# Cross-attention with layer norm on one Trainium2 core: the mask conversion on GpSimd in pieces, other staging of the weights, and another order of the end

## The chip, the cores and the metric

The kernel runs on one core of a Trainium2 chip. A core has five engines with instruction queues of their own: PE (TensorE, matmuls; its weight loads are shown as PEld), DVE (VectorE), ACT (ScalarE), POOL (GpSimd) and SP (SyncE, which here only issues transfers). Each engine works through its queue in order, and semaphores tie the queues together. Sixteen DMA engines move data between the main memory (HBM), the on-chip memory (SBUF) and within SBUF. PE writes its results to PSUM, which has 8 banks here. The metric is the device time of one execution in microseconds.

## What is computed

```python
qs = (x @ wq) split into 16 heads of 32        # x: 4 x 2048 x 512
ks, vs = ctx @ wk, ctx @ wv                    # ctx: 4 x 77 x 512
scores = einsum("bhqd,bhkd->bhqk", qs, ks) / sqrt(32)
scores = where(mask, -inf, scores)             # mask: 4 x 2048 x 77
attn = softmax(scores) @ vs                    # heads joined again
out = attn @ wo + x
return (out - mean) / sqrt(var + 1e-5) * gamma + beta
```

All tensors are float32, the mask is one byte for each query and key. A query whose 77 keys are all masked must come out as NaN.

## The kernel before

**Tiles.** The 8192 queries are 64 tiles of 128 rows, 16 tiles a batch. Two tiles make a block (32 blocks, each with one attention-times-values group), four tiles a group for the query projection (16 groups). Keys are 77 wide, or 96 (NK2) with a copy of the last 19 so that two neighbouring heads can lie at different offsets.

**Precision.** Projections are done as three products of a high and a low part (`split`: ACT rounds the high part, DVE or GpSimd subtracts). So x, wq, wk, wo, wv, the context and the attention output all exist as high and low tiles.

**The main loop.** One period (`PERIOD`, lines 45 to 50) is a list of words that is recorded once for each p from 0 to 29; each word names an operation and, behind the colon, its lag. One period handles two tiles: two Q visits on PE (`Q`, line 168, 12 matmuls each) with their evacuation by DVE (`q`, line 185), scores of two tiles (`S`, line 291), maxima with the mask bias added (`T`, DVE, line 305, four quarters a tile), exponentials (`e`, ACT, line 319), reciprocals (`r`, DVE, line 330), normalisation (`n`, POOL, line 335), transposes into a B buffer (`t`, DVE, line 359), regrouping of B into PT by twelve DMAs a block (`P`, line 371, parts 0 to 11, in this loop all on SP), attention times values (`V`, line 385), its high and low parts (`a`, ACT, line 416; `b`, DVE, line 420), output projection (`O`, line 440), residual (`+`, DVE, line 449), statistics (`s`, lines 454 to 457), inverse deviation (`v`, POOL, lines 463 to 466), scaling (`k`, ACT), gamma and beta (`f`, POOL, lines 476 and 477) and store (`w`, SP). `g`, `i` and `j` load, round (ACT, line 157) and subtract (POOL, line 161) the transposed x of a group; `x` loads x for the residual.

**Extras.** The dictionary `extra` (lines 608 to 622) hangs further calls behind a word of a certain period: values projections, splits of wv and wo, and the mask. `load_mask` (line 263) fetches a batch's mask bytes into m8, which has one buffer, and takes the bias tile mb (two buffers). `mask_bias` (line 270) turns the bytes into a bias of -3e38 or 0 in bf16: one DVE multiplication, line 272, and a DVE copy of the 19 repeated columns, line 273. `mask_nan` (line 275) reduces the mask to one value a query that is NaN where all keys are masked, lines 277 to 279. For batch m the first tiles run in period p = 2 + 8m; the load hangs at p - 3, the two halves of the bias at p - 2 and p - 1, the NaN row at p - 1. Batch 0 is loaded at the start; its bias is made in three slices (lines 555, 610 and 611), its NaN row in period 5.

**Buffers.** The staging tiles stage_a and stage_b and all PT tiles share the tag PT (two buffers); ctx_f, ctx_h (context as loaded, and its high part) and all B tiles share the tag B (two buffers). stage_a takes wq and wk, then xT of group 1; stage_b takes wv and wo. ctx_h is read by the keys and the values projections.

**Order.** The kernel is recorded under a manual schedule: each engine's queue holds its instructions in the order in which the words and extras call them. After period 29 the string `ORDER` (lines 52 to 72) takes over and lists the rest word by word, with the queue of each regroup transfer (s SP, g GpSimd, a ACT). There, `U` is a regroup of a single tile, `X` adds the residual by an identity matmul on PE (line 429) in place of `+`, and `u`, `y`, `z` are the steps of the layer norm for one tile.

```python
 extra[p - 3, "S0"] = [(load_mask, m)]
 extra[p - 2, "T1.1"] = [(mask_bias, m, slice(0, half))]
 extra[p - 1, "T1.1"] = [(mask_bias, m, slice(half, TPB)), (mask_nan, m)]
```

Of the kernel before, what the change touches and what calls it, by code (L numbers as in the profile page):

```python
# [57 lines left out]
P27.0s n56 Q60 q61 e57.1 P27.5s T58.3 P27.6s b25.1 e58.3 q62 P27.11g T58.2 S59 u48 x55 e57.3 t56 Q63 P27.1g
e58.2 r57 T59.0 n57 T59.1 e59.0 q60 T59.2 V26 e59.1 f46 T59.3 t57 e58.1 O50 q63 P28.4g a26.0 w46 z48 a26.1
P28.8s P28.7g b26.0 e58.0 P28.10g P28.0s z49 S60 P28.3g b26.1 e59.2 P28.2g +50 O53 P28.6g x54 r58 T60.1 w49 n58  # L60
e59.3 w48 T60.3 P28.9s T60.0 e60.3 T60.2 S61 t58 e60.1 X51 x57 P28.11s r59 T61.2 n59 e60.0 V27 P28.1s T61.0
P28.5s T61.1 e61.2 +53 O51 t59 e60.2 T61.3 P29.3g P29.11s s50 x56 S62 P29.2s a27.0 r60 u50 s51 e61.1 P29.8s O52
T62.0 P29.6s u51 b27.0 a27.1 P29.10s e61.3 T62.1 P29.9s P29.0g y51 b27.1 n60 e61.0 V28 +52 T62.2 r61 S63 T62.3
P29.4g a28.0 t60 a28.1 n61 X55 e62.1 b28.0 O55 P29.5a s52 e62.2 t61 u52 X54 e62.3 P29.7g b28.1 P30.2s P30.3g z51
X57 P30.8s P29.1g P30.4a T63.2 P30.1s O54 y52 P30.6s e62.0 T63.3 P30.11s T63.0 P30.0s e63.3 y50 w51 O57 r62 z50
P30.10s P30.7a T63.1 n62 w50 s53 e63.0 s54 V29 x59 P30.9a P30.5g z52 e63.1 t62 u53 O56 a29.1 y53 U62.5g U62.9s
U62.10a h63.0 U62.8s s55 m63.0 e63.2 x58 b29.1 w52 V30 z53 a29.0 h63.1 w53 U62.3a y55 s57 m63.1 U62.4a X59 b29.0
u55 a30.1 t63 a30.0 O59 U62.0a x61 y57 U63.6g U63.4s U62.11a y54 U62.1s U63.1a b30.0 u54 U62.6s O58 +56 U63.11s
U63.9a U63.10g b30.1 U63.5a U63.7g x60 z55 U63.3g z54 w55 O61 U63.0s s56 u57 U63.2s +58 U63.8g U62.7s z57 U62.2s
s58 u56 O60 x63 w54 +61 u58 s59 s61 u59 W63 +60 u61 x62 s60 W62 c63 w57 y59 X63 c62 d63 u60 d62 O63 y61 y58 z61  # L70
y60 X62 y56 z60 O62 z58 w60 w61 z56 w58 s63 z59 s62 u63 w59 w56 y63 u62 y62 z63 z62 w63 w62
"""


# [1 line left out]
def xattn_layernorm(  # L76
# [186 lines left out]
    def load_mask(b):
        m8 = sb.tile([P, TPB, NK], U8, tag="m8", bufs=1, name=f"m8_{b}")
        nc.sync.dma_start(m8, mask[b])
        mb = sb.tile([P, TPB, NK2], BF16, tag="mb", name=f"mb_{b}")
        nz = sb.tile([P, TPB], F32, tag="nz", name=f"nz_{b}")
        bat[b] = (mb, nz, m8)

    def mask_bias(b, ts=slice(0, TPB)):  # L270
        mb, nz, m8 = bat[b]
        nc.vector.tensor_scalar(mb[:, ts, TAIL_K:], m8[:, ts], MASKED, None, ALU.mult)
        nc.vector.tensor_copy(mb[:, ts, :TAIL_K], mb[:, ts, NK:])

    def mask_nan(b):
        mb, nz, m8 = bat[b]
        nc.vector.tensor_reduce(nz, m8, AX.X, ALU.min)
# [274 lines left out]
    for c in range(0, NC_D, 2):  # L552
        split(*(a[:, c : c + 2, BLK:] for a in gx[0]), f0[c][:, 1])
    q_visit(0, 0)
    mask_bias(0, slice(0, 1))
    gate(stage_a[:, 1, NC_D - 1, D - 1 :])
    load_wv()
    for m in range(0, NG, 2):
        keys_evac(pks, m)
# [58 lines left out]
    for m in range(1, NB):
        p = 2 + m * half
        extra[p - 3, "S0"] = [(load_mask, m)]  # L620
        extra[p - 2, "T1.1"] = [(mask_bias, m, slice(0, half))]
# [65 lines left out]
```

## Time and profile before

| | |
|---|---|
| median of 3 runs | 549.29 us (548.66 to 549.4) |
| the profiled execution | 549.31 us, its span 547.5 us |
| mean granted clock of PE | 0.982 of full speed |
| ACT, exponentials, 1024 (line 319) | 352.7 us busy, 351 ns each |
| DVE, maxima, 1024 (line 305) | 170.5 us busy, 232 ns each |
| DVE, transposes, 64 (line 359) | 96.2 us busy, 1503 ns each |
| POOL, normalisation, 63 (line 335) | 142.6 us busy, 2264 ns each |
| DVE, mask bias, 616 elements (line 272) | 6 of 770 ns |
| DVE, mask bias, 152 elements (line 273) | 6 of 1188 ns |
| DVE, NaN reduction (line 277) | 4 of 1421 ns |

The span runs from the first to the last instruction of the program in one execution; the execution's own time is a little longer. Busy time is the union of an engine's instructions. In the tables by stage, each row is one stretch of the span: its length, then the busy time of each engine in it with the number of instructions, then the mean granted clock of PE and the share of the DMA engines. In the timeline, each line has the start, the duration, the engine ("SPq" is SP's queue issuing transfers), the line of the kernel, what is written and read, how many, and in brackets the idle time of the engine before it and what ended it.

### The profile page before, as it was taken

What the parts mean: (1) busy time and instruction counts of PE and PEld (TensorE: products, weight loads), DVE (VectorE), ACT (ScalarE), POOL (GpSimd) and SP (SyncE); (2) the same over time, 40 slices, a digit from 0 to 9 for tenths busy, and PEclk for the clock granted to TensorE, in tenths of its full rate; (3) what the DMA queues carried; (4) which work ended last, traced back from release to release, by engine and by line L of the source; (5) the groups of instructions that cost most, each with busy time, mean ns of one, the idle gap of its engine ahead of it and who ended that gap; (6) DMA issues with size and microseconds to landing.
All of it is one profiled execution on the core that took longest, in us unless ns stands there. A gap on an engine that the chain in (4) does not pass through costs nothing.

```text
span 547.5 us, 16162 instructions
## 1 busy us (share of the span) xinstructions
PE 529.8 (97%) x4809; PEld 410.4 (75%) x4809; DVE 488.3 (89%) x2600; ACT 461.0 (84%) x2215; POOL 402.7 (74%) x367
## 2 busy tenths in 40 slices
PE   8998989999999999999999999999999999999994
PEld 6976677777877777777777777777777777776573
DVE  5795688899898888899998888899998889899997
ACT  6697576998989999998999999998999999898500
POOL 0544155887888888887988888887988899767561
PEclk9998979999899999999999999999999999999998
DMA  8933367655768776765877876765877775875964
GB/s 307 402 112 74 119 188 195 162 167 171 227 198 231 215 216 193 215 177 166 247 211 229 229 198 196 216 177 168 241 214 228 227 208 146 193 210 155 254 190 157
DMA packets 58567, 109.96 MB, mean 201 GB/s; under 512 B 9392, under 2 KB 11056, under 8 KB 58480
## 3 DMA queue, kind: packets, MB, share of 16 engines
q1 hardware_dynamic: 55024, 102.12, 63.3%
q0 software_dynamic: 2496, 5.77, 3.9%
q10 hardware_dynamic: 960, 1.05, 0.7%
q8 instruction: 38, 0.62, 0.5%
q14 instruction: 49, 0.40, 0.3%
HBM read 41.79 MB, written 16.78 MB: 107 GB/s over the span
## 4 chain that ended last, share of the span: by engine, by line
PE 51%; DVE 27%; DMA 8%; POOL 7%; SPq 4%; issue 3%; ACT 0%; DVEq 0%; ACTq 0%; POOLq 0%
PE pq L168 20%; PE po L440 17%; PE sc L291 7%; DVE pbuf L305 7%; DVE B L359 6%; DMA PT<-B 5%; PE pa L385 5%; POOL pbuf L335 2%; SPq L371 2%; DVE q L185 2%; DMA stage_b<-wo 2%; DVE o L449 2%; POOL o L476 1%; DVE AL L420 1%; POOL o L477 1%
## 5 line engine op out<-in xcount | busy, mean ns | idle before, releaser
L319 ACT ACTIVATE pbuf<-pbuf,nm 128x77 f32<-128x77 f32 x1024 | 352.7, 351 | 31.7 <-DVE nm L305 19.8
L319 ACT ACTIVATION_READ_ACCUMULATOR pbuf<-pbuf,nm 128x1 f32 x1024 | 195.6, 191 | 0.0
L335 POOL TENSOR_TENSOR pbuf<-pbuf,ri 128x1232 f32<-128x1232 f32 x63 | 142.6, 2264 | 63.5 <-DVE ri L330 48.0
L305 DVE CUSTOM_DVE_ANT_0 pbuf<-sc,mb 128x77 f32<-128x77 f32 x1024 | 170.5, 232 | 11.7 <-PE sc L291 8.0
L359 DVE STREAM_TRANSPOSE B<-pbuf 128x1280 f32<-128x1280 f32 x64 | 96.2, 1503 | 8.2 <-DMA PT<-B 8.1
L168 PE MATMUL pq<-xth,wqh 128*128 128x512 f32 (+1 forms) x256 | 102.6, 401 | 0.0
L440 PE MATMUL po<-woh,AH 128*128 128x512 f32 x256 | 102.5, 400 | 0.0
L440 PE MATMUL po<-woh,AL 128*128 128x512 f32 x256 | 99.8, 390 | 0.9 <-DVE AL L420 0.9
L440 PE MATMUL po<-wol,AH 128*128 128x512 f32 x256 | 99.7, 390 | 0.0
L168 PE MATMUL pq<-xth,wql 128*128 128x512 f32 (+1 forms) x256 | 99.3, 388 | 0.0
L168 PE MATMUL pq<-xtl,wqh 128*128 128x512 f32 (+1 forms) x256 | 99.2, 387 | 0.0
L291 PEld LDWEIGHTS sc<-kct,q 32*128 32x128 f32 x2048 | 69.1, 190 | 32.7 <-issue 13.7
L291 PE MATMUL sc<-kct,q 32*128 32x77 f32 x2048 | 80.6, 282 | 7.5 <-DVE q L185 4.6
L305 DVE DVE_READ_ACCUMULATOR2_ANT nm<- 128x1 f32 x1024 | 84.3, 82 | 0.1
L161 POOL TENSOR_TENSOR xtl<-xtf,xth 128x1024 fp32r<-128x1024 f32 x28 | 66.5, 2375 | 0.0
L477 POOL TENSOR_TENSOR o<-o,bet 128x512 f32<-128x512 f32 x48 | 62.2, 1296 | 3.8
L476 POOL TENSOR_TENSOR o<-o,gam 128x512 f32<-128x512 f32 x48 | 63.7, 1327 | 0.0
L385 PE MATMUL pa<-PT,vsb 96*32 96x256 f32 x992 | 60.0, 382 | 0.3 <-issue 0.3
L440 PEld LDWEIGHTS po<-woh,AH 128*128 128x128 f32 x256 | 48.1, 188 | 12.6 <-issue 2.0
L168 PEld LDWEIGHTS pq<-xth,wqh 128*128 128x128 f32 x256 | 48.9, 191 | 11.4 <-DVE nm L305 0.4
L440 PEld LDWEIGHTS po<-woh,AL 128*128 128x128 f32 x256 | 48.1, 188 | 11.4 <-DVE AL L420 1.3
L168 PEld LDWEIGHTS pq<-xth,wql 128*128 128x128 f32 x256 | 48.8, 191 | 10.2
(99 smaller groups left out, 672.4 us busy)
## 6 DMA issues: line engine op xcount, KB each, us to landing
PT<-B SPq DMA_DIRECT2D x343, 128.0 KB, 2.8
o<-x SPq DMA_DIRECT2D x64, 256.0 KB, 3.8
out<-o SPq DMA_DIRECT2D x64, 256.0 KB, 2.5
xtf<-xT SPq DMA_DIRECT2D x28, 512.0 KB, 4.0
PT<-B POOLq DMA_DIRECT2D x25, 128.0 KB, 3.6
xtf<-xT SPq DMA_DIRECT2D x4, 256.0 KB, 4.8
stage_a<-wq SPq DMA_DIRECT2D x4, 256.0 KB, 4.7
stage_a<-wk SPq DMA_DIRECT2D x4, 256.0 KB, 6.3
```

The costliest lines, as they stand in the source:

```text
L161: nc.gpsimd.tensor_tensor(l, fx.pop((g, c)), h.bitcast(F32), ALU.subtract)
L168: nc.tensor.matmul(pq, w[:, c, m * P : (m + 1) * P], r[:, c, rs], start=(n == 0), stop=(n == 11))
L185: nc.vector.tensor_copy(qd[g][:, m, :], pq)
L291: nc.tensor.matmul(sc[j][:, g * NK : (g + 1) * NK], qs[q, g, rs], kct[q, g, t // TPB, keys_of(j)], start=True, stop=True,)
L305: nc.vector.tensor_tensor_reduce(pb[:, h // 2, (h % 2) * NK : (h % 2 + 1) * NK], scs[t][j][:, g * NK : (g + 1) * NK], mb[:, t % TPB, keys_ ...
L319: nc.scalar.activation(pb[:, h // 2, (h % 2) * NK : (h % 2 + 1) * NK], pb[:, h // 2, (h % 2) * NK : (h % 2 + 1) * NK], AF.Exp, bias=nmax[t ...
L335: nc.gpsimd.tensor_tensor(pv, pv, rv.to_broadcast((P, NP, 2, NK)), ALU.mult)
L359: nc.vector.transpose(bt.rearrange("p c q r -> p q c r"), pbuf[t % NPB].rearrange("p q (c r) -> p q c r", c=5),)
L385: nc.tensor.matmul(pas[b, g // 2][HD * j : HD * (j + 1), (g % 2) * BLK : (g % 2 + 1) * BLK], vsb[:, 2 * b // TPB, HD * h : HD * (h + 1)], ...
L440: nc.tensor.matmul(pos[t], a[:, c, rs], w[:, c, :], start=(first and c == 0 and n == 0), stop=(c == NC_D - 1 and n == 2),)
L476: nc.gpsimd.tensor_tensor(o, o, gam, ALU.mult)
L477: nc.gpsimd.tensor_tensor(o, o, bet, ALU.add)
```

## The change

- **Mask.** The bias is computed by GpSimd instead of DVE, from the bytes in both cases (no copy of the repeated columns), in four pieces of four tiles for each of batches 1 to 3, behind the normalisation word n0 of the periods p - 5 to p - 2. Batch 0: the first tile's slice stays on DVE, the other two slices go to GpSimd in period 2. The load of the mask moves from period p - 3 to p - 6, and the NaN row comes in two halves of eight tiles, behind r0 of the periods p - 2 and p - 1; for batch 0 both halves stand behind r0 of period 5.
- **Staging.** stage_b is gone. wv lands in the second half of stage_a (where wk was), wo in the first half (where wq and then xT of group 1 were). load_wv is called behind the loads of xT of group 1. All four wo splits stand in period 4.
- **Context.** The high part of the context is a view of a new tile stage_c, which shares the tag PT; so only ctx_f and the B tiles share the tag B.
- **The rest.** Ten warm-up matmuls instead of nine; the string ORDER is another one (nine X and seven + instead of eight each; 14, 46 and 29 regroup transfers on ACT, SP and GpSimd instead of 12, 46 and 31).

```diff
-WARM = 9
+WARM = 10
...
-P25.5s T55.0 e54.3 P25.11s T55.2 O48 T55.1 k47 r54 q59 n54 e55.2 t53 S56 e55.0 +48 P26.0s f47 X49 T55.3 P26.2s
+P25.5g P25.8s f44 e53.1 Q59 P25.9s t52 P25.11s a24.1 P25.3s r53 T55.2 e54.0 n53 g31 T55.1 Q58 T54.3 e54.2 b24.1
...
-    stage_b = sb.tile([P, 2, NC_D, D], F32, tag="PT", name="stage_b")
+    stage_c = sb.tile([P, 2, NC_D, D], F32R, tag="PT", name="stage_c")
     ctx_f = sb.tile([P, NC_D, NB, NK2], F32, tag="B", name="ctx_f")
-    ctx_h = sb.tile([P, NC_D, NB, NK2], F32R, tag="B", name="ctx_h")
+    ctx_h = stage_c[:, 0][:, :, : NB * NK2].rearrange("p c (b k) -> p c b k", b=NB)
...
-            nc.sync.dma_start(stage_b[:, 0, c], wview(wv, c))
+            nc.sync.dma_start(stage_a[:, 1, c], wview(wv, c))
...
-            nc.sync.dma_start(stage_b[:, 1, c], wview(wo, c))
+            nc.sync.dma_start(stage_a[:, 0, c], wview(wo, c))
...
-        nz = sb.tile([P, TPB], F32, tag="nz", name=f"nz_{b}")
-        bat[b] = (mb, nz, m8)
-
-    def mask_bias(b, ts=slice(0, TPB)):
+        bat[b] = [mb, None, m8]
+
+    def mask_bias(b, ts, eng=nc.gpsimd):
+        mb, _, m8 = bat[b]
+        eng.tensor_scalar(mb[:, ts, TAIL_K:], m8[:, ts], MASKED, None, ALU.mult)
+        eng.tensor_scalar(mb[:, ts, :TAIL_K], m8[:, ts, NK - TAIL_K :], MASKED, None, ALU.mult)
+
+    def mask_nan(b, i):
+        if i == 0:
+            bat[b][1] = sb.tile([P, TPB], F32, tag="nz", name=f"nz_{b}")
         mb, nz, m8 = bat[b]
-        nc.vector.tensor_scalar(mb[:, ts, TAIL_K:], m8[:, ts], MASKED, None, ALU.mult)
-        nc.vector.tensor_copy(mb[:, ts, :TAIL_K], mb[:, ts, NK:])
-
-    def mask_nan(b):
-        mb, nz, m8 = bat[b]
-        nc.vector.tensor_reduce(nz, m8, AX.X, ALU.min)
-        nc.vector.tensor_scalar(nz, nz, 3.0e38, 10.0, ALU.mult, ALU.mult)
-        nc.vector.tensor_scalar(nz, nz, 0.0, EPS, ALU.mult, ALU.add)
+        ts = slice(i * TPB // 2, (i + 1) * TPB // 2)
+        nc.vector.tensor_reduce(nz[:, ts], m8[:, ts], AX.X, ALU.min)
+        nc.vector.tensor_scalar(nz[:, ts], nz[:, ts], 3.0e38, 10.0, ALU.mult, ALU.mult)
+        nc.vector.tensor_scalar(nz[:, ts], nz[:, ts], 0.0, EPS, ALU.mult, ALU.add)
...
-    mask_bias(0, slice(0, 1))
+    mask_bias(0, slice(0, 1), nc.vector)
...
-        (2, "S1"): [(q_visit, 0, 2), (load_wo,), (idents,)],
-        (3, "T0.3"): [(mask_bias, 0, slice(1, 2))],
-        (3, "T1.1"): [(q_evac, 0, 2), (split_wv,), (mask_bias, 0, slice(2, TPB))],
+        (2, "S1"): [(q_visit, 0, 2), (mask_bias, 0, slice(1, 2)), (mask_bias, 0, slice(2, TPB)), (load_wo,), (idents,)],
+        (3, "T1.1"): [(q_evac, 0, 2), (split_wv,)],
         (3, "S1"): [(values, 0), (values, 1)],
-        (4, "T1.1"): [(values_evac, 0), (values_evac, 1), (split_wo, 0), (split_wo, 1)],
+        (4, "T1.1"): [(values_evac, 0), (values_evac, 1)] + [(split_wo, c) for c in range(NC_D)],
         (4, "S1"): [(values, 2), (values, 3)],
-        (5, "T1.1"): [(values_evac, 2), (values_evac, 3), (split_wo, 2), (split_wo, 3), (mask_nan, 0)],
+        (5, "T1.1"): [(values_evac, 2), (values_evac, 3)],
+        (5, "r0"): [(mask_nan, 0, 0), (mask_nan, 0, 1)],
     }
-    half = TPB // 2
+    quarter = TPB // 4
     for m in range(1, NB):
-        p = 2 + m * half
-        extra[p - 3, "S0"] = [(load_mask, m)]
-        extra[p - 2, "T1.1"] = [(mask_bias, m, slice(0, half))]
-        extra[p - 1, "T1.1"] = [(mask_bias, m, slice(half, TPB)), (mask_nan, m)]
+        p = 2 + m * TPB // 2
+        extra[p - 6, "S0"] = [(load_mask, m)]
+        for i in range(4):
+            extra[p - 5 + i, "n0"] = [(mask_bias, m, slice(i * quarter, (i + 1) * quarter))]
+        for i in range(2):
+            extra[p - 2 + i, "r0"] = [(mask_nan, m, i)]
```

More of the change, by code (lines that the diff above doesn't have):

```diff
@@ L52 @@
 ORDER = """
-f44 g31 Q58 a24.1 P25.8s b24.0 e53.1 t52 P25.3g e54.0 T54.3 v23 x53 Q59 P25.9s q58 e54.2 r53 w44 b24.1 n53
-P25.5s T55.0 e54.3 P25.11s T55.2 O48 T55.1 k47 r54 q59 n54 e55.2 t53 S56 e55.0 +48 P26.0s f47 X49 T55.3 P26.2s
-e55.1 T56.0 P26.11s O49 T56.2 P26.3s i31 t54 P26.1s P26.10g e55.3 P26.5s j31 T56.1 P26.9s S57 T56.3 e56.0 r55
-s49 V25 n55 e56.1 T57.0 T57.3 Q61 k46 T57.2 P26.8g a25.0 y49 e56.2 P26.7g T57.1 u49 t55 a25.1 S58 e57.2 P26.6g
-s48 P27.9s P27.8g Q62 w47 P27.10g T58.0 e56.3 P27.4s P27.3g b25.0 P27.7s P26.4g y48 e57.0 x52 P27.2g r56 T58.1
@@ L58 @@
[L58 to L71, printed above, removed]
+P25.5g P25.8s f44 e53.1 Q59 P25.9s t52 P25.11s a24.1 P25.3s r53 T55.2 e54.0 n53 g31 T55.1 Q58 T54.3 e54.2 b24.1
@@ new lines @@
+v23 b24.0 e54.3 T55.0 O48 q59 e55.0 T55.3 q58 e55.2 r54 t53 n54 S56 i31 +48 P26.8s O49 e55.1 T56.1 P26.7s
+P26.10g T56.2 P26.1s P26.2g T56.0 e55.3 j31 x53 t54 P26.11s P26.3s S57 k47 P26.9s +49 e56.1 V25 P26.6g w44 r55
+T56.3 P26.0g P26.4s e56.0 s48 n55 Q61 T57.2 e56.2 T57.0 x52 T57.1 P26.5g e56.3 T57.3 u48 t55 S58 a25.0 e57.2 Q60
+r56 P27.0g P27.3s y48 P27.4s b25.0 n56 e57.0 T58.3 P27.1s q61 P27.10s a25.1 T58.0 Q63 P27.2s e57.3 P27.7g T58.1
+P27.5s P27.9g T58.2 P27.11s P27.6g e57.1 b25.1 z48 S59 e58.1 r57 t56 n57 V26 e58.0 q60 T59.3 f47 k46 X50 q63
@@ new lines @@
+a26.0 T59.2 Q62 e58.2 t57 a26.1 w47 T59.1 P28.7g e59.3 P28.6s T59.0 f46 P28.1s O50 s49 e59.2 P27.8s q62 x55
+b26.0 e58.3 P28.3s P28.9g y49 S60 P28.8s s50 u49 e59.1 P28.10s X51 b26.1 P28.2g w46 T60.2 e59.0 P28.0s O51 z49
+r58 w49 y50 P28.11a T60.0 n58 e60.2 T60.1 x54 P28.5s S61 T60.3 w48 s51 e60.3 u50 V27 P28.4s t58 e60.1 u51 X52
+r59 T61.1 x57 n59 e60.0 T61.2 O52 T61.3 e61.2 T61.0 y51 a27.0 t59 a27.1 X53 e61.3 r60 S62 P29.6g P29.8s b27.0
+n60 s52 e61.1 P29.0s O53 P29.10s T62.2 P29.9s P29.11a b27.1 P29.4s T62.1 P29.3g e61.0 z51 O55 T62.0 w51 e62.2
@@ new lines @@
+x56 y52 P29.7s r61 s53 n61 e62.0 P29.1s t60 V28 e62.1 P29.2g y53 P29.5g x59 T62.3 S63 a28.0 u53 +55 a28.1 X54
+e62.3 t61 u52 X57 b28.0 P30.4a P30.3s P30.2g O54 b28.1 P30.0s P30.7g P30.11a T63.1 P30.8g P30.6s r62 P30.10a z50
+P30.9g z53 w50 e63.1 V29 P30.5s T63.0 n62 T63.3 w53 e63.0 P30.1s s54 O56 s55 u54 a29.0 x58 e63.3 T63.2 h63.0 t62
+m63.0 a29.1 O57 e63.2 b29.1 U62.7g U62.9s z52 U62.2g U62.11a x61 y54 U62.6s U62.5a h63.1 b29.0 w52 m63.1 V30 s57
+u55 t63 O59 a30.0 U62.10g a30.1 y55 U63.9s U63.11g U62.1a +56 u57 U62.8s U62.3a b30.0 x60 U63.6s O58 z55 U63.2g
@@ L72 @@
+U63.5a U62.4g z54 w55 U62.0a U63.0s y57 w54 s56 U63.4a U63.7s X61 b30.1 u56 U63.3a +58 x63 O61 U63.1a y56 U63.8g
+U63.10g z57 z56 w57 s58 O60 +59 u58 x62 s61 y58 s59 u61 W62 +60 u59 W63 c62 s60 X62 c63 y61 d62 u60 X63 d63 O62
+y59 z61 y60 z59 z60 O63 w59 z58 w60 w56 s62 w58 w61 y62 u62 s63 y63 u63 z62 z63 w62 w63
 """
@@ L249, in split_wv @@
         for c in range(NC_D):
-            nc.vector.tensor_tensor(wvl[c], stage_b[:, 0, c], wvh[c].bitcast(F32), ALU.subtract)
+            nc.vector.tensor_tensor(wvl[c], stage_a[:, 1, c], wvh[c].bitcast(F32), ALU.subtract)
     def load_wo():
         for c in range(NC_D):
-            nc.sync.dma_start(stage_b[:, 1, c], wview(wo, c))
+            nc.sync.dma_start(stage_a[:, 0, c], wview(wo, c))
         nc.gpsimd.dma_start(woh, wo.rearrange("(c p) e -> p c e", p=P))
@@ L259, in split_wo @@
     def split_wo(c):
-        nc.vector.tensor_tensor(wol[:, c], stage_b[:, 1, c], woh[:, c].bitcast(F32), ALU.subtract)
+        nc.vector.tensor_tensor(wol[:, c], stage_a[:, 0, c], woh[:, c].bitcast(F32), ALU.subtract)
     def load_mask(b):
@@ L554, in xattn_layernorm @@
     q_visit(0, 0)
-    mask_bias(0, slice(0, 1))
+    mask_bias(0, slice(0, 1), nc.vector)
     gate(stage_a[:, 1, NC_D - 1, D - 1 :])
-    load_wv()
     for m in range(0, NG, 2):
@@ L562, in xattn_layernorm @@
         nc.sync.dma_start(fx[1, c], xT[1, :, c : c + 2])
+    load_wv()
     for c in range(0, NC_D, 2):
```

## The prediction

> **What bounds the kernel now.** I read the shares on the page first, then the busy time by stage, then the timeline of PE and of DVE where a stage is slow. A difference of 0.2% (1.1 us) is about what a measurement of this kernel can tell from no change.
>
> ```profile
> PE 529.8 (97%) x4809; PEld 410.4 (75%) x4809; DVE 488.3 (89%) x2600; ACT 461.0 (84%) x2215; POOL 402.7 (74%) x367
> core 0: us, PE busy (x) PEld busy (x) DVE busy (x) ACT busy (x) POOL busy (x), PEclk, DMA share, GB/s
> 64.93:80.93 16.00, 13.51 (x121) 10.51 (x121) 13.78 (x78) 11.32 (x63) 6.85 (x3) 0.79 0.51 135
> 119.60:138.04 18.44, 17.54 (x180) 13.75 (x176) 18.09 (x94) 15.64 (x75) 14.55 (x12) 1.00 0.60 176
> 138.04:153.15 15.11, 15.11 (x105) 11.89 (x108) 12.46 (x69) 13.28 (x65) 13.39 (x12) 0.89 0.78 236
> 451.88:547.50 95.62, 86.83 (x769) 62.51 (x767) 89.01 (x387) 59.40 (x305) 60.46 (x79) 0.98 0.66 186
> ```
>
> An undisturbed period takes 15.11 us and PE never rests in it; DVE is left 2.65 us of idle time, GpSimd 1.72. So an edit is worth only what it does to the few places where PE waits. From the starts of PE's groups there are five. In period 4 (46.3 to 59.4) the scores wait for the Q evacuation and the clock falls: 5.4 us. In period 5 (66.0 to 80.9): 6.4 us. In the second mask period of each later batch, at 119.6 to 145, 244 to 263 and 367 to 386: 3.9, 2.25 and 2.25 us, 8.4 together. The last three begin on DVE:
>
> ```profile
> 127.12 0.78 DVE L272 TENSOR_SCALAR mb<-m 128x616 bf16<-128x616 uint8 x1
> 127.93 1.18 DVE L273 COPY mb<-mb 128x152 bf16<-128x152 bf16 x1
> 129.03 1.42 DVE L277 TENSOR_REDUCE nz<-m 128x16 f32<-128x1232 uint8 x1
> ...
> 135.74 0.44 PE L291 MATMUL sc<-kct,q 32*128 32x77 f32 x2 [0.53 <-DVE o L449]
> 136.37 0.44 PE L291 MATMUL sc<-kct,q 32*128 32x77 f32 x2 [0.18 <-DVE nm L305]
> 137.00 1.11 PE L291 MATMUL sc<-kct,q 32*128 32x77 f32 x26 [0.19 <-DVE nm L305]
> ```
>
> The mask rows put 3.7 us (127.12 to 130.78) ahead of DVE's evacuations, more than its idle 2.65, and the scores find no free bank. Period 5 is different:
>
> ```profile
> 48.52 3.94 SPq L371 DMA_DIRECT2D PT<-B  x6
> 52.51 0.59 SPq L425 DMA_DIRECT2D o<-x  x1
> 53.14 4.03 SPq L371 DMA_DIRECT2D PT<-B  x6
> ...
> 56.57 2.42 DMA PT<-B
> ...
> 59.27 1.51 DVE L359 STREAM_TRANSPOSE B<-pbuf 128x1280 f32<-128x1280 f32 x1 [6.67 <-DMA PT<-B]
> ...
> 70.82 3.36 PE L291 MATMUL sc<-kct,q 32*128 32x77 f32 x30 [1.55 <-DVE q L185]
> ```
>
> Block 0's twelve regroup transfers land at 59.0. Tile 2's transpose writes the same B buffer and waits 6.67 us for them; everything after it on DVE is late, and PE waits at 66 to 71.
>
> **The start.** One more warm-up matmul costs one pitch, 0.43 us, but PE's third projection matmul waits for DVE's wql until 5.58 anyway: 0, at most 0.3. The weights in staging halves keep their bytes. wv must wait for wk's splits (last at 15.4), wo for GpSimd's subtraction of group 1 (25.3); their users run at 29.3 and 42.5, so with the 8.3 us that wo took to land there is cover, and 0 is taken. Leaving the mask rows 0.71 and 0.24 off DVE at 31.74 brings the Q evacuations forward; the 64 score matmuls at 32.63 took 2.49 us against 64 x 33 ns = 2.1: 0.4 us gained. Tile 1's bias, now on GpSimd behind the subtraction that ends at 25.3, is needed at 25.9 and may be 0.3 late on a DVE that is idle 2.66 us at 43.7: 0. The four wo splits together (4 x 0.6) fall before that idle end too. Period 4's wait for q1, transpose, q0 is untouched.
>
> **Period 5, the step that decides.** With ctx_h outside tag B, tile 2's transpose needs no landing any more; tile 4's does, a period later. But the mask of batch 1 is now loaded in period 4, into the one m8 buffer, which mask_nan(0) reads in period 5 behind r0. In the changed program's SP queue this load stands behind three of block 0's twelve regroups and waits for DVE's second reduction. Queued behind it: nine regroups that the first AV group needs, two x loads, xtf of group 3, then block 1. Its time: PE finishes the Q visits at 64.93 - 0.4 = 64.5; then DVE does q1, transpose, q0, reciprocal (0.1 + 0.60 + 1.43 + 0.58 + 0.16, starts at 46.39 to 49.0 and 70.69), half a reduction 0.75, two small rows 0.42, the second half 0.75: 69.3. SP then needs 0.08 and 0.49 for the mask load (pitch at 101.18), 3 regroups x 0.665, 0.63 for x, 5 x 0.67 up to the last issue, and 2.42 to land: 9.0 us. AV starts at 78.3 instead of 66.0; PE is idle for some 12 us.
>
> After it come AV (1.86 at full clock; at half by the pitch of a 512-column matmul, 427 to 231 ns, 3.4), scores (1.06; 1.7 at the 52 ns of the slow stretch at 49.1) and two Q visits (5.6; 6.83 after the stall of before; up to 7.3). The ends for the output projection are 78.3 + 8.5 = 86.8 and 78.3 + 12.4 = 90.7; but ACT's cast of xtf group 3, landing near 80.5, holds 3 quarters of exps (1.37 each) and two AH casts, so AL is there no sooner than 88. I take 78.3 + 2.6 + 1.5 + 6.83 = 89.2. Before, it began at 80.93: +8.3, bounds +7 and +9.8.
>
> The clock decides within these bounds: in the profile's own rows it stayed at half for 6.83, 6.83 and 3.41 us after the three waits that lowered it, twice for a second window although PE was working. The Trainium skill (TensorE: Matmul & The Clock Gate, What's actually happening) says full clock after one busy window of about 3.4 us; by it the projection would begin near 89, by the two-window rows at 90.7.
>
> **The mask batches.** Per batch, DVE loses 2 x (0.77 + 1.19) and keeps the reduction in two halves of 0.75 + 0.35 to 0.42, 1.15 us in each of two periods, set behind r0. There DVE is idle 1.08 us before the second residual and 0.37 before the maxima (at 150.88 and 151.94), so it is covered; uncovered it would be the 1.15. All 8.4 us go: -8.4 (bounds -8.4 and -6).
>
> GpSimd gets four pieces of 308 + 76 elements per batch. No row shows such an operation. Below: two of its smallest rows, 2 x 0.197 = 0.4 us. Above: two of the 0.507 copy and 384 elements at L161's 2.3 ns, 1.9 us. I take 1.3, nearest to L161's pace. They stand before L161's subtraction (150.58 to 152.94), whose result Q needs at 154.76: 1.8 us of cover, so 0; at the upper bound 0.1 in six periods.
>
> The Trainium skill speaks against it: GPSIMD Engine Reference, Specifications, has GpSimd share its SBUF interfaces with VectorE when that runs a two-port mode or reads two SBUF inputs. A row agrees: L273 took 1188 ns for 152 elements beside a busy GpSimd and 243 for 266 beside an idle one. By the row the change also removes the worst case; by the rule a piece could be stretched by such a wait, and the sum would be the slow rival's.
>
> **The end.** From 451.88 PE works almost without a rest (1.3 us idle, 0.88 of it at 518.6 for AL). Nine identity residuals instead of eight: 2 x 0.28 + 0.4 of switching = +0.9. After PE's last matmul (539.96) DVE still had 4.45 us to do, 0.9 of it backlog; in the new order six rows instead of nine lie between the last AL and the last statistics: three rows of 0.66 would be 2, of which I count 1.0, about the backlog. Of the 1.3 us of waits I count half, 0.7. Sum +0.9 - 1.0 - 0.7 = -0.8; bounds -2.5 and +2, since no row shows the new order.
>
> **Sum.** 549.31 (the profiled execution, span 547.5 and 1.8 around it; the median of the runs is 549.29) + 8.3 - 8.4 - 0.8 = 548.4 us. The gain of the masks is spent in period 5.
>
> **Rivals.** (A) *The mask load does not hold up SP*, for instance because AV is covered. For it: xtf and x loads sit in the same queue at no cost today. Against it: AV needs all twelve parts. Period 5 would then be bound by DVE: maxima after the reductions, 69.7 + 1.3 = 71.0, scores 1.7, Q 6.83: projection at 79.5, -1.4. 549.31 - 1.4 - 8.4 - 0.8 = 538.7. (B) *GpSimd becomes the bound in the mask periods*: if its two rows of a piece are held as L273 was (0.95 each), a piece takes 1.3 + 1.9 = 3.2; over 1.8 the subtraction is late for Q, in the two even periods of each of three batches: 6 x 1.4 = +8.4, 556.8. It decides from 1.8 us a piece. Against it: the engine holding L273 was GpSimd, not the other way. (C) *The new end is worse*: transposes or regroups come late for AV 26 to 30. At +3 instead of -0.8: 552.2. For it: DVE is busy 89 of 95.6 us there.
>
> **Chances.** Forecast 0.66 (its own range 546.9 to 550.7; 0.28 faster, 0.25 same, 0.13 slower), A 0.14, B 0.08, C 0.12. So faster 0.42, same 0.25, slower 0.33. The range 545.0 to 552.4 leaves out A, B and a little of the ends.
>
> **What would show it.** Right: SP's mask load issues near 69 with nine regroups behind it, AV starts at 77 to 79, the projection of period 6 at 88 to 91, and PE's periods from there to 446 are all 15.1 us. Wrong: AV at 66 to 72 (A); a GpSimd piece over 1.8 us and Q waiting for xtl (B); PE gaps after the cut (C); or scores waiting for DVE in the periods with half a reduction.

## The result and the profile after

The changed kernel took 574.38 us in the median of 4 runs (573.23 to 575.62), the kernel before 549.35 (4 runs, 548.66 to 549.50): a ratio of 1.0459 with a 95% interval of 1.0434 to 1.0483. It is 25 us slower, where 548.4 was predicted and 552.4 was the top of the range. In the later comparisons the kernel before itself took 548.4 to 557.3 us, in two groups 6 to 7 us apart (and once 650), so an experiment's ratio is given with its interval, and the readings rest on the stretches of its profile.

The profiled execution has a span of 573.8 us against 547.5. The first line is the busy time on the page; the others are busy time by stage, with the columns named in the second line:

```profile
PE 539.7 (94%) x4812; PEld 416.9 (73%) x4812; DVE 498.7 (87%) x2595; ACT 461.2 (80%) x2215; POOL 419.4 (73%) x393
core 0: us, PE busy (x) PEld busy (x) DVE busy (x) ACT busy (x) POOL busy (x), PEclk, DMA share, GB/s
64.69:93.64 28.95, 14.18 (x122) 10.42 (x121) 14.54 (x78) 12.02 (x62) 8.21 (x5) 0.65 0.66 174
93.64:477.68 384.04, 377.22 (x3458) 294.18 (x3456) 348.00 (x1881) 343.58 (x1645) 325.96 (x283) 0.98 0.67 195
140.06:161.65 21.59, 19.56 (x145) 15.13 (x144) 19.06 (x93) 17.61 (x89) 16.17 (x14) 0.84 0.51 154
477.68:573.80 96.12, 87.23 (x771) 62.95 (x769) 90.91 (x381) 59.63 (x305) 57.72 (x76) 0.99 0.65 190
```

DVE is busier by 10.4 us although the mask bias has left it. The stretches account for the whole difference:

| stretch | before | after | difference | predicted |
|---|---|---|---|---|
| start to the scores of period 5 | 64.93 | 64.69 | -0.2 | -0.4 |
| from there to the projection of period 6 | 16.00 | 28.95 | +12.95 | +8.3 with the start |
| 24 periods, projection of 6 to that of 30 | 370.95 | 384.04 | +13.1 | -8.4 |
| from there to the end | 95.62 | 96.12 | +0.5 | -0.8 |

Two places lose 13 us each. The first is the queue of SP in period 5. These are SP's transfers in the timeline of the changed kernel (start, duration, what is fetched, how many):

```profile
48.29 2.02 SPq L373 DMA_DIRECT2D PT<-B  x3
71.04 0.34 SPq L265 DMA_DIRECT2D m<-mask  x1
71.42 1.87 SPq L373 DMA_DIRECT2D PT<-B  x3
73.34 0.58 SPq L427 DMA_DIRECT2D o<-x  x1
73.97 3.79 SPq L373 DMA_DIRECT2D PT<-B  x6
```

Three of block 0's twelve regroups go out at 48.3; then SP rests until the mask load can go at 71.04, and only behind it come the other nine. PE starts the first AV group (attention times values) at 80.59. The page of waits says what this costs PE and, in its wake, ACT and DVE (line and awaited transfer: total, times, longest):

```profile
ACT xth L157 <- DMA xtf<-xT: 21.9, 1, 21.9
PE pa L387 <- DMA PT<-B: 14.8, 1, 14.8
DVE B L361 <- DMA PT<-B: 6.6, 1, 6.6
```

The second place is DVE in the two periods of each batch that hold half a NaN reduction. The timeline of DVE, and then of GpSimd, in the second such period of batch 1:

```profile
143.62 0.74 DVE L279 TENSOR_REDUCE nz<-m 128x8 f32<-128x616 uint8 x1
144.39 1.79 DVE L280 TENSOR_SCALAR nz<-nz 128x8 f32<-128x8 f32 x1
146.21 2.29 DVE L281 TENSOR_SCALAR nz<-nz 128x8 f32<-128x8 f32 x1
148.41 0.68 DVE L451 TENSOR_TENSOR o<-po,o 128x512 f32<-128x512 f32 x1
...
143.90 2.25 POOL L337 TENSOR_TENSOR pbuf<-pbuf,ri 128x1232 f32<-128x1232 f32 x1
146.11 2.36 POOL L161 TENSOR_TENSOR xtl<-xtf,xth 128x1024 fp32r<-128x1024 f32 x1
```

The reduction takes the 0.74 us that were foreseen. The two rows of eight numbers behind it take 1.79 and 2.29. The first ends at 146.18, when GpSimd's normalisation ends (146.15), the second at 148.50, when its subtraction ends (148.47). The residual (L451) that would follow at 144.7 by the old prices of the rows comes at 148.4; the scores find no bank, and this period lasts, from one output projection to the next, 21.59 us (the 140.06 row above) in place of 15.11, with the clock down to 0.84; the first of the two periods, from 123.85 on, lasts 16.21. In the groups of all instructions (busy us, mean ns of one):

```profile
L280 DVE TENSOR_SCALAR nz<-nz 128x8 f32<-128x8 f32 x8 | 12.6, 1573 | 0.3
L281 DVE TENSOR_SCALAR nz<-nz 128x8 f32<-128x8 f32 x8 | 8.3, 1042 | 0.3
```

In the kernel before, rows of twice as many elements took 0.17 us each. GpSimd rested there for 3.27 us, up to 133.69 (DVE, then GpSimd, in the timeline of the kernel before):

```profile
130.48 0.17 DVE L278 TENSOR_SCALAR nz<-nz 128x16 f32<-128x16 f32 x1
130.69 0.17 DVE L279 TENSOR_SCALAR nz<-nz 128x16 f32<-128x16 f32 x1
...
133.69 2.25 POOL L335 TENSOR_TENSOR pbuf<-pbuf,ri 128x1232 f32<-128x1232 f32 x1 [3.27 <-DVE ri L330]
```

### The profile page after: what moved, and what is told of

Same layout as the page of the kernel before. It is cut to its first block, busy times and chain, and to the rows that moved or that the text cites. A ratio compares the mean times of both kernels' runs of the same rounds, so it can differ in the third digit from the quotient of the medians.

```text
span 573.8 us, 16212 instructions
## 1 busy us (share of the span) xinstructions
PE 539.7 (94%) x4812; PEld 416.9 (73%) x4812; DVE 498.7 (87%) x2595; ACT 461.2 (80%) x2215; POOL 419.4 (73%) x393
## 4 chain that ended last, share of the span: by engine, by line
PE 60%; DVE 27%; DMA 3%; POOL 3%; issue 2%; SPq 2%; DVEq 0%; ACT 0%
PE pq L168 25%; PE po L442 17%; PE sc L293 9%; DVE pbuf L307 6%; PE pa L387 6%; DVE B L361 5%; PE pv L229 2%; DVE AL L422 2%; DVE q L185 2%; DVE nz L280 2%; DVE o L498 2%; DVE o L501 2%; DVE o L451 2%; SPq L373 2%; DMA PT<-B 1%
## 5 line engine op out<-in xcount | busy, mean ns | idle before, releaser
L307 DVE CUSTOM_DVE_ANT_0 pbuf<-sc,mb 128x77 f32<-128x77 f32 x1024 | 170.7, 234 | 15.4 <-PE sc L293 11.8
L168 PE MATMUL pq<-xth,wqh 128*128 128x512 f32 (+1 forms) x256 | 105.7, 413 | 0.0
L168 PE MATMUL pq<-xtl,wqh 128*128 128x512 f32 (+1 forms) x256 | 101.2, 395 | 0.0
L168 PE MATMUL pq<-xth,wql 128*128 128x512 f32 (+1 forms) x256 | 101.1, 395 | 0.0
L293 PEld LDWEIGHTS sc<-kct,q 32*128 32x128 f32 x2048 | 70.5, 193 | 36.2 <-issue 12.5
L293 PE MATMUL sc<-kct,q 32*128 32x77 f32 x2048 | 82.4, 285 | 9.7 <-DVE o L451 5.0
L307 DVE DVE_READ_ACCUMULATOR2_ANT nm<- 128x1 f32 x1024 | 85.7, 84 | 0.1
L387 PE MATMUL pa<-PT,vsb 96*32 96x256 f32 x992 | 61.7, 390 | 15.1 <-DMA PT<-B 14.8
L478 POOL TENSOR_TENSOR o<-o,gam 128x512 f32<-128x512 f32 x48 | 62.2, 1296 | 0.0
L168 PEld LDWEIGHTS pq<-xth,wql 128*128 128x128 f32 x256 | 50.1, 196 | 10.8
L168 PEld LDWEIGHTS pq<-xtl,wqh 128*128 128x128 f32 x256 | 50.4, 197 | 9.5 <-issue 0.2
L442 PEld LDWEIGHTS po<-woh,AH 128*128 128x128 f32 x256 | 48.0, 188 | 11.8 <-issue 2.0
```

The lines of the kernel that those rows point to most:

```text
L168: nc.tensor.matmul(pq, w[:, c, m * P : (m + 1) * P], r[:, c, rs], start=(n == 0), stop=(n == 11))
L293: nc.tensor.matmul(sc[j][:, g * NK : (g + 1) * NK], qs[q, g, rs], kct[q, g, t // TPB, keys_of(j)], start=True, stop=True,)
L307: nc.vector.tensor_tensor_reduce(pb[:, h // 2, (h % 2) * NK : (h % 2 + 1) * NK], scs[t][j][:, g * NK : (g + 1) * NK], mb[:, t % TPB, keys_ ...
L387: nc.tensor.matmul(pas[b, g // 2][HD * j : HD * (j + 1), (g % 2) * BLK : (g % 2 + 1) * BLK], vsb[:, 2 * b // TPB, HD * h : HD * (h + 1)], ...
L442: nc.tensor.matmul(pos[t], a[:, c, rs], w[:, c, :], start=(first and c == 0 and n == 0), stop=(c == NC_D - 1 and n == 2),)
L478: nc.gpsimd.tensor_tensor(o, o, gam, ALU.mult)
```

## The experiments

The theory after the result has two parts: the NaN rows wait for GpSimd (13 us over the batches against before, 21 against undisturbed periods), and the mask load blocks SP's queue in period 5. The rivals: GpSimd's pieces, the halved reductions, the context's new place or the new end.

**The NaN rows at a place where GpSimd rests.**

```diff
-        nc.vector.tensor_scalar(nz[:, ts], nz[:, ts], 3.0e38, 10.0, ALU.mult, ALU.mult)
-        nc.vector.tensor_scalar(nz[:, ts], nz[:, ts], 0.0, EPS, ALU.mult, ALU.add)
+    def nan_rows(b):
+        nz = bat[b][1]
+        nc.vector.tensor_scalar(nz, nz, 3.0e38, 10.0, ALU.mult, ALU.mult)
+        nc.vector.tensor_scalar(nz, nz, 0.0, EPS, ALU.mult, ALU.add)
...
+        (5, "S1"): [(nan_rows, 0)],
+        extra[p - 1, "S1"] = [(nan_rows, m)]
```

> The changed kernel with one thing moved: the two small NaN rows (L280, L281) leave their place behind the reductions and are done once per batch, over all 16 tiles, behind the scores of the last tile of the same period, where GpSimd rests between its subtraction and the next rn (199.86 to 201.45 in the changed kernel's trace). Reductions, mask pieces, loads and order stay. Theory: in the changed kernel the rows last until the GpSimd instruction that runs beside them ends (1573 and 1042 ns in the mean), and this is what costs 21.4 us in the three later batches and 1.9 us in period 5. Then the rows take 0.17 to 0.4 us each here, the 24 periods from the projection of period 6 on fall from 384.0 us to 363 to 366, and the time is 574.4 - 21.4 - 1.9 = 551, between 549 and 555. Rival: the reductions in two halves or GpSimd's mask pieces hold up the scores: then most of the 21.4 stays and the time is 568 to 574, with rows as short as before.

Measured: 550.61 us (10 runs, 546.52 to 553.25), ratio 0.9979 [0.9934, 1.0023]. The stage of the 24 periods, and DVE's rows in its timeline:

```profile
90.87:453.43 362.56, 362.56 (x3458) 284.01 (x3457) 331.06 (x1875) 343.60 (x1651) 326.25 (x283) 1.00 0.72 207
...
139.36 0.73 DVE L279 TENSOR_REDUCE nz<-m 128x8 f32<-128x616 uint8 x1
140.01 0.67 DVE L454 TENSOR_TENSOR o<-po,o 128x512 f32<-128x512 f32 x1
...
144.79 0.17 DVE L283 TENSOR_SCALAR nz<-nz 128x16 f32<-128x16 f32 x1
144.99 0.18 DVE L284 TENSOR_SCALAR nz<-nz 128x16 f32<-128x16 f32 x1
```

In 362.56 us PE is busy for 362.56 at clock 1.00: not one wait is left. All 21.5 us of the batches came from the two rows; reductions and GpSimd pieces stand where they stood and cost nothing. The rival falls.

**The mask load behind the reduction that frees its buffer.**

```diff
-        (5, "r0"): [(mask_nan, 0, 0), (mask_nan, 0, 1)],
+        (5, "r0"): [(mask_nan, 0, 0), (mask_nan, 0, 1), (load_mask, 1)],
...
-        extra[p - 6, "S0"] = [(load_mask, m)]
+        if m > 1:
+            extra[p - 6, "S0"] = [(load_mask, m)]
```

> The changed kernel with the load of batch 1's mask alone moved: from the end of period 4 to period 5, behind mask_nan(0), so that no regroup transfer of block 0 stands behind it in SP's queue. Theory: the blocked queue is what period 5 lost 12.7 us to. Then all twelve regroups of block 0 are issued by 53, AV starts near 68 to 70 instead of 80.6, the projection of period 6 near 81 (93.64 - 12 = 81.6), and the time is 574.4 - 12 = 562.4, between 560 and 565; the batches stay as slow as they are. Rival: period 5 is late because of the NaN rows on DVE (1.9 us) and the reductions: then the projection comes at 91 or later and the time is 571 to 574.

Measured: 561.43 us (4 runs, 560.65 to 562.53), ratio 1.0171 [1.0098, 1.0243]. SP's timeline in this kernel:

```profile
48.42 3.94 SPq L373 DMA_DIRECT2D PT<-B  x6
...
53.03 3.80 SPq L373 DMA_DIRECT2D PT<-B  x6
...
67.99 0.33 SPq L265 DMA_DIRECT2D m<-mask  x1
```

The regroups are out by 56.8 and the mask load still waits until 67.99, with nothing of block 0 behind it. The projection of period 6 starts at 78.87 in place of 93.64. AV starts at 62.76, not at the expected 68 to 70. Of these 14.8 us, 11.8 lie in period 5; the other 3.0 lie before it (its scores start at 61.69 instead of 64.69), a difference that executions of equal code show as well (last section). The batches stay slow (383.87 us).

**Both moves together.**

> Both moves together. If the two causes are independent and are the whole loss, the gains add: 574.4 - 23.3 - 12 = 539, between 536 and 542, some 10 us under the kernel before, because ctx_h's place and the masks on GpSimd then bring what they can (period 5 at its DVE bound, no waits in the batches). If something else of the change costs (mask pieces, staging, the new end), it stays above 546.

Measured: 538.04 us (4 runs, 536.42 to 540.86), ratio 0.9751 [0.9676, 0.9826]; the projection of period 6 at 75.47, the 24 periods 362.56. The two gains, 23.8 and 12.95, would add up to 36.7; 36.3 were measured. So the two gains add up, as far as the spread of the runs lets one see, and between them the two causes are the whole loss and more: what is left of the change is a gain of 11 us.

**Is it the port that the two engines share?** The same rows at the same places, in a form that also writes a sum.

```diff
-        nc.vector.tensor_scalar(nz[:, ts], nz[:, ts], 3.0e38, 10.0, ALU.mult, ALU.mult)
+        nc.vector.tensor_scalar(nz[:, ts], nz[:, ts], 3.0e38, 10.0, ALU.mult, ALU.mult, accum_out=ac[:, 0:1])
...
```

> The changed kernel with the NaN rows in their places, but in the form that also writes a sum of its output (into a small tile of its own; the added EPS may be missing in this form, so the output can differ in its last digits). By the Trainium skill (SBUF — State Buffer, section on what contends) that form of tensor_scalar does not enter the two-port mode, and so should not wait for GpSimd. Theory (the wait is for the port pair that the two engines share): the rows beside L337 and L161 take 0.2 to 0.4 us in place of 1.8 and 2.3, and the time comes to 549 to 553 as in e1_rows_idle. Rival (any DVE row that reads what a row just before it wrote, at this place, waits for GpSimd): the rows keep 1.8 and 2.3 us, and the time 573 to 576.

Measured: 551.73 us (one run), the 24 periods 362.56. DVE and then GpSimd in the timeline:

```profile
140.48 0.17 DVE L281 TENSOR_SCALAR_CACHE_REDUCE nz<-nz 128x8 f32<-128x8 f32 x1
140.56 0.09 DVE L281 DVE_READ_ACCUMULATOR nz<-nz 128x1 f32 x1
140.69 0.16 DVE L282 TENSOR_SCALAR_CACHE_REDUCE nz<-nz 128x8 f32<-128x8 f32 x1
...
139.99 2.27 POOL L338 TENSOR_TENSOR pbuf<-pbuf,ri 128x1232 f32<-128x1232 f32 x1
```

In the midst of GpSimd's 2.27 us row, both DVE rows take 0.17, and all sixteen such rows of this execution took 161 to 165 ns. Place, input and neighbour are those of the changed kernel; the form alone decides. That a shared port is what lies behind it is not visible in a trace. The Trainium skill (SBUF — State Buffer, Who interferes with whom) states the rule: a DVE copy or `tensor_scalar` that can run in a mode with two ports takes the pair of ports that GpSimd uses, whoever comes second waits for the other's whole instruction, and the form that writes out its accumulator doesn't enter that mode. The rows of both kernels agree: 1.79 us in the one form, 0.17 in the other.

**The mask pieces on DVE, at the same places.** This is `e3_both` with one word changed; batch 0's two later slices move to DVE with it.

```diff
-    def mask_bias(b, ts, eng=nc.gpsimd):
+    def mask_bias(b, ts, eng=nc.vector):
```

> e3_both with the four mask pieces of each batch on DVE in place of GpSimd, at the same places. By DVE's 616-element row (0.78 us) a piece of 308 and 76 elements takes some 0.4 + 0.17 = 0.6 us there; DVE rests 1.08 us before the second residual and 0.37 before the maxima. Theory: cutting the mask into pieces is what ends the waits of the batches, not the engine: 538.0, between 537 and 540, the 24 periods from 75.47 on still near 362.6. Rival: DVE has no room at this place and the scores come late in 12 periods: 0.3 to 0.6 us each, 542 to 545.

Measured: 587.54 us (4 runs, 583.09 to 590.77), ratio 1.0581 [1.0460, 1.0702], 50 us off the expectation and beyond its rival too. The 24 periods took 409.22 us. The timeline shows the misjudgement, the same one as in the prediction:

```profile
87.11 2.09 DVE L271 TENSOR_SCALAR mb<-m 128x308 bf16<-128x308 uint8 x1
89.12 2.36 DVE L272 TENSOR_SCALAR mb<-m 128x76 bf16<-128x76 uint8 x1
...
86.77 2.26 POOL L340 TENSOR_TENSOR pbuf<-pbuf,ri 128x1232 f32<-128x1232 f32 x1 [5.35 <-DVE ri L335]
88.98 2.43 POOL L161 TENSOR_TENSOR xtl<-xtf,xth 128x1024 fp32r<-128x1024 f32 x1
```

Both rows of a piece last until GpSimd's row ends (89.20 for 89.03, 91.48 for 91.41): 4.4 us for work that was priced at 0.6.

**The same pieces in the form with a sum**, with the old order of the end (`e5_both_old_order`, below).

```diff
-        eng.tensor_scalar(mb[:, ts, TAIL_K:], m8[:, ts], MASKED, None, ALU.mult)
+        nc.vector.tensor_scalar(mb[:, ts, TAIL_K:], m8[:, ts], MASKED, 0.0, ALU.mult, ALU.add, accum_out=ac[:, 0:1])
...
```

> e5_both_old_order with the four mask pieces of each batch on DVE, as in e8_pieces_dve, but in the form that also writes a sum. Theory (e8's 50 us were waits for the port pair, up to 2.4 us a row): the two rows of a piece take about 0.4 + 0.2 us, DVE's rest at this place covers them but for a little, and the time is 535.8 to 540. Rival (DVE has no room for any row at this place): 12 periods are late by 0.6 us and more, the clock falls, and the time is 545 or more.

Measured: 542.03 us (4 runs, 540.31 to 543.43), ratio 0.9805 [0.9724, 0.9885], between the two forecasts. By stage and in DVE's timeline:

```profile
83.21:445.77 362.56, 362.56 (x3458) 284.07 (x3456) 335.50 (x1912) 341.69 (x1641) 310.99 (x261) 1.00 0.72 208
...
71.79 0.47 DVE L272 TENSOR_SCALAR_CACHE_REDUCE mb<-m 128x308 bf16<-128x308 uint8 x1 [2.23 <-DMA m<-mask]
86.74 0.46 DVE L272 TENSOR_SCALAR_CACHE_REDUCE mb<-m 128x308 bf16<-128x308 uint8 x1
```

In the batches DVE does cover the pieces, all of them. The 6.43 us that are lost lie before 83.21 (76.78 in `e5_both_old_order`, with the pieces on GpSimd). In period 5 the first piece stands on DVE in front of the maxima and waits 2.23 us there for the mask, which the moved load fetches only then; PE's wait for the maxima grows from 1.61 to 4.47 us, and the granted clock from 61 us to the projection falls from 1.00 to 0.85. Another 0.7 us are already there when the scores of period 5 start (65.27 for 64.55). So GpSimd is the better place for the piece that waits for a transfer; for the others DVE would have done, in this form.

**Did the kernel before pay for the port too?** Its two mask rows in that form, the second one made from the bytes instead of the copy.

```diff
-        nc.vector.tensor_scalar(mb[:, ts, TAIL_K:], m8[:, ts], MASKED, None, ALU.mult)
-        nc.vector.tensor_copy(mb[:, ts, :TAIL_K], mb[:, ts, NK:])
+        nc.vector.tensor_scalar(mb[:, ts, TAIL_K:], m8[:, ts], MASKED, 0.0, ALU.mult, ALU.add, accum_out=ac[:, 0:1])
+        nc.vector.tensor_scalar(mb[:, ts, :TAIL_K], m8[:, ts, NK - TAIL_K :], MASKED, 0.0, ALU.mult, ALU.add, accum_out=ac[:, 1:2])
```

> The kernel before, at its own places on DVE, with its two mask rows (L272, L273) in the form that also writes a sum of its output, and the second one made from the uint8 mask in place of the copy. Nothing else is changed. Theory (the rows waited for GpSimd there too: 0.78 and 1.19 us beside its rows, where 1155 elements beside an idle GpSimd took 0.71): a half batch then takes about 0.75 + 0.30 = 1.05 us in place of 1.96, the second mask period holds 2.8 us of mask work against DVE's idle 2.65, and of the 8.4 us that the three batches lose 4.5 to 7.5 come back: the 24 periods from the projection of period 6 on fall from 370.95 to 363.5 to 366.5, and the time to 542 to 545. Rival (DVE simply has too much work in that period, 3.7 us in whatever form): 548 to 551.

Measured: 547.91 us (10 runs, 546.00 to 548.89), ratio 0.9915 [0.9869, 0.9960]; the 24 periods 368.24 against 370.95. DVE and then GpSimd in the timeline:

```profile
128.19 0.79 DVE L273 TENSOR_SCALAR_CACHE_REDUCE mb<-m 128x616 bf16<-128x616 uint8 x1
128.91 0.31 DVE L274 TENSOR_SCALAR_CACHE_REDUCE mb<-m 128x152 bf16<-128x152 uint8 x1
129.14 1.43 DVE L278 TENSOR_REDUCE nz<-m 128x16 f32<-128x1232 uint8 x1
130.61 0.69 DVE L279 TENSOR_SCALAR nz<-nz 128x16 f32<-128x16 f32 x1
...
129.97 1.29 POOL L478 TENSOR_TENSOR o<-o,bet 128x512 f32<-128x512 f32 x1
```

The second mask row falls from 1.18 us to 0.31 as expected. But DVE comes 0.9 us sooner to the NaN rows, GpSimd's L478 is still running there, and the first NaN row, left in the old form, now waits: 0.69 in place of 0.17, in all three batches. A wait that is removed brings the next row of the same kind beside the same engine.

Only 2.7 us came back, where 4.5 to 7.5 were expected, and the new wait accounts for at most 1.5 of what is missing (3 x 0.5). The three second mask periods last 16.48, 16.49 and 18.04 us here and 18.92, 17.29 and 17.28 before, against 15.11 undisturbed; in each execution the clock falls in the longest of the three. The other two are 0.8 us shorter here. The forecast set the mask work against 2.65 us of idle time of DVE, but an undisturbed period has 1.51 (next section). The mask work is 3.2 us here (128.19 to 131.41) and 3.7 before: 1.7 and 2.2 us more than that, and the periods without a fall of the clock are 1.4 and 2.2 us longer than undisturbed. So the rival, too much work on DVE in that period, accounts for most of what remains, and the time lies just under its 548 to 551. (The forecast's 1155 elements are 1078 in the row of the trace.)

**The context's place alone.** `e3_both` with ctx_h under tag B again.

```diff
-    ctx_h = stage_c[:, 0][:, :, : NB * NK2].rearrange("p c (b k) -> p c b k", b=NB)
+    ctx_h = sb.tile([P, NC_D, NB, NK2], F32R, tag="B", name="ctx_h")
```

> e3_both with the context's high part back under tag B, as in the kernel before. Theory: tile 2's transpose waits some 6.7 us again for the landing of block 0's regroup transfers (about 59), so period 5 is late: the projection of period 6 starts at 79.5 to 81 in place of 75.47, and the time is 542 to 543.5. Rival: the wait is covered by PE's own work in period 5 (as the prediction's rival A had it, -1.4 us only): then 538 to 540.

Measured: 540.69 us (4 runs, 539.97 to 541.97), ratio 0.9764 [0.9688, 0.9841]. DVE's timeline has the old wait again:

```profile
59.49 1.51 DVE L364 STREAM_TRANSPOSE B<-pbuf 128x1280 f32<-128x1280 f32 x1 [7.20 <-DMA PT<-B]
```

The projection starts at 81.02 in place of 75.47, at the top of the expected span; the median rose by 2.7, which lies between the two forecasts of the time. The 5.5 us of the profiled pair compare the fastest run of `e3_both` (536.42) with the slowest of this kernel (541.97). By the medians the edit is worth about 3 us.

**The end.** Twice: the kernel before with the new order, and `e3_both` with the old one (and its nine warm-up matmuls).

> The kernel before with only the new order of the end (the text behind the cut at period 30). By the two traces the stretch from the cut's first Q to the end took 95.62 before and 96.1 in the changed kernel: +0.5, so 549.8, between 549 and 551. The prediction's term was -0.8: 548.5. Rival C of the prediction gave +3: 552.3.

> Both moves of e3_both, and the end in the order of the kernel before (with its nine warm-up matmuls). The stretch from the cut's projection to the end took 95.62 us in the kernel before and 96.57 in e3_both: if the order makes that difference, the time is 538.0 - 0.95 = 537.1, between 536 and 538. If the new order is as good or better, it is 538 to 540.

Measured: the kernel before with the new order 555.25 us (10 runs, 549.55 to 557.92), ratio 1.0049 [0.9996, 1.0102], which does not tell it from no change. The median lies above the expected 549 to 551; the ten runs spread over 8 us, as those of the kernel before do. Its profile gives the stretch itself, 96.18 us. `e5_both_old_order` took 535.84 us (4 runs, 535.35 to 536.92), just under the expected 536 to 538, ratio 0.9677 [0.9601, 0.9752], with 95.66 us for the end:

```profile
439.34:535.00 95.66, 87.02 (x769) 62.52 (x767) 88.89 (x387) 59.35 (x305) 60.47 (x79) 0.97 0.68 189
```

So the new order takes 96.1 to 96.6 us in the profiles of all eight kernels that have it, the old one 95.4 to 95.7 in all four: 0.5 to 1.2 us worse. `e5_both_old_order` is the fastest version found by its median, 13.5 us under the kernel before by the medians 549.35 and 535.84, which are from different comparisons; its own interval is the better measure.

## Why the prediction was wrong

- **The start.** -0.2 for -0.4, but not by the reason given. The 64 score matmuls, which were to gain the 0.4, take 2.49 us up to the next matmul as before (32.39 to 34.88; before, 32.63 to 35.12); the 0.24 us are already there when they begin, and where they come from is open. So the near agreement is chance. The staging in halves costs nothing that the trace shows.
- **Period 5, called the step that decides.** The mechanism was right in each link: the load behind three regroups, the wait for the second reduction, nine regroups behind it, then AV. The size was too small: the projection came 12.7 us later than before (93.64 for 80.93), where +8.3 was the term and +9.8 its bound. AV started 2.3 us after the calculated 78.3, mostly since the first NaN row took 1.73 us and the load went at 71.04, not 69.3; without that row, in `e1_rows_idle`, the load goes at 69.30 and the projection comes at 90.87, close to the upper bound of 90.7. From AV to the projection it took 13.05 us in place of 10.9, since the half clock lasted longer (last section). This term alone, at +12.7, would have put the time at 552.8, just above the range.
- **The mask batches: the step that failed.** It read: "keeps the reduction in two halves of 0.75 + 0.35 to 0.42, 1.15 us in each of two periods, set behind r0. There DVE is idle 1.08 us before the second residual and 0.37 before the maxima (at 150.88 and 151.94), so it is covered". The reduction took 0.74, but the rows 2.2 us in the first of the two periods (1.82 + 0.37 in batch 1) and 4.1 in the second. Their price came from rows beside a resting GpSimd; behind r0 the next thing GpSimd does is n0, the normalisation that r0 releases. The move itself put them beside the engine they wait for. With the rows elsewhere the term was right to the tenth: 370.95 - 362.56 = 8.4 us.
- **The idle time of DVE was misread.** The row taken for an undisturbed period (138.04 to 153.15) is none: it begins inside the second mask period, holds 105 matmuls of PE, where a period has about 145, and has clock 0.89. A period from one output projection to the next, without mask work, in the kernel before (busy time by stage):

```profile
175.45:190.56 15.11, 15.11 (x145) 11.83 (x144) 13.60 (x81) 14.41 (x71) 13.17 (x12) 1.00 0.75 217
```

  DVE is left 1.51 us in it, not 2.65, and GpSimd 1.94, not 1.72. The half reduction with its rows, at the 1.15 us that were priced, would still have fitted.
- **The evidence was in the prediction.** It set L273's 1188 ns beside 243 ns for more elements, said that the change "removes the worst case", and looked for harm only to GpSimd's pieces (rival B, 556.8). It did not ask which DVE instructions the change leaves in that form, and beside what.
- **GpSimd's pieces.** 0.99 + 0.40 = 1.39 us, predicted 1.3, and covered as predicted. Rival B did not come about.
- **The end.** +0.5 in place of -0.8, within its bounds (-2.5 and +2) and on the other side. Rival C had the sign and a size (+3) that is too large.
- **The rivals.** A (period 5 not held up, 538.7) has the time that `e3_both` makes of the change, 538.04, but partly by chance: A counted -1.4 us for period 5 and -0.8 for the end, where the profile of `e3_both` shows -5.5 (75.47 for 80.93) and +1.0 (96.57 for 95.62), and its own time is 536.42. None of the cases held two losses at once, and the price of the NaN rows had no upper bound: had each of the twelve later rows been given GpSimd's longest row (2.4 us) as its upper bound, 12 x 2.2 = 26 us would have stood above the forecast, at 575. That this bound meets the measured 574.4 is chance: by the rows the batches lost 21.5 us, and period 5 lost 4.4 beyond its term.

## What to carry to other kernels

Price a small DVE copy or `tensor_scalar` by what GpSimd does beside it at the new place, not by its size: in the plain form it may last as long as GpSimd's instruction, and the form that also writes a sum does not. Before a load is moved forward in a queue, look for the buffer it must wait for and count what stands behind it in that queue. When a stall of this kind is taken away, look at the next instruction of the same form, which now starts at another time.

## What was not expected of the hardware

- A row of 8 numbers a partition took up to 2.30 us. Not every GpSimd instruction holds it to its end: beside the mask piece (L271, one input, bytes to bf16, 0.98 us) that started 0.1 us earlier (129.55 for 129.64 in batch 1), L281 took 0.37 us, three times out of three. Why it was let through is open; the spans of GpSimd are rough.
- The half clock outlasts the wait. After the 14.8 us of period 5 PE worked without a pause, and yet the clock stayed low for another 9.73 us (busy time by stage, changed kernel):

```profile
64.69:80.59 15.90, 1.13 (x33) 1.01 (x33) 9.03 (x43) 0.00 (x0) 3.60 (x3) 0.66 0.48 133
80.59:90.32 9.73, 9.73 (x74) 6.70 (x75) 5.51 (x36) 8.70 (x43) 4.61 (x2) 0.50 1.01 250
90.32:93.64 3.32, 3.32 (x16) 2.71 (x15) 0.00 (x0) 3.32 (x21) 0.00 (x0) 1.00 0.48 151
```

  The Trainium skill (TensorE: Matmul & The Clock Gate, What's actually happening) has full clock after about one busy window of 3.4 us. Here the AV and score groups (5.5 us; their matmuls are 96*32 and 32*128 in the timeline, not 128*128) and 4.2 us of the query projection went by first. Which of them failed to count was not tried.
- Equal code does not always take equal time. The kernel before and `e4_order_only` are the same up to the cut. Their stretch from the scores of period 4 to those of period 5, and their 24 periods, are here by stage, the first two lines from the one and the last two from the other (two fences):

```profile
46.28:64.93 18.65, 16.49 (x114) 12.48 (x113) 10.98 (x74) 10.69 (x58) 6.85 (x3) 0.82 0.52 142
80.93:451.88 370.95, 368.26 (x3457) 288.01 (x3456) 340.78 (x1877) 343.27 (x1645) 312.34 (x261) 1.00 0.71 205
```

```profile
46.33:62.52 16.19, 13.43 (x113) 10.26 (x112) 7.75 (x46) 7.47 (x44) 4.62 (x2) 1.00 0.59 162
82.32:459.72 377.40, 374.71 (x3457) 292.83 (x3456) 341.29 (x1884) 343.06 (x1641) 313.06 (x261) 0.98 0.70 201
```

  The waits are alike, but in the one execution the clock fell behind period 4's wait and not in the other (0.82, 1.00), and in the batches it was the other way round. In the batches the second mask periods of batches 2 and 3 take 20.46 and 20.45 us there, 17.29 and 17.28 before. By these pairs a single profile of such a kernel is uncertain by some 2 to 3 us at each wait that can lower the clock.
